# Cross attention with an adapter on one core: the wait of the turns of Wq, halves of columns in the last text unit, and a new order of all operations

## The chip, the cores and the metric

The kernel runs on one core of a Trainium2 chip. A core has five engines with instruction streams of their own: TensorE (PE in the profile, its weight loads are PEld), VectorE (DVE), ScalarE (ACT), GpSimd (POOL) and SyncE (SP), which here only issues DMAs. ACT and POOL issue DMAs too. Each engine works through its stream in order; semaphores hold it until what it needs is done. The metric is the device time of one execution in microseconds, the median of several. Lower is better.

## The reference

All is fp32. x is (2, 2048, 640), the context is (2, 128, 384): 124 text tokens and 4 adapter tokens `ca` for each batch. There are 8 heads of 80.

```python
enc, ca = context[:, :124], context[:, 124:]
query = x @ Wq                                    # (2, 2048, 640)
hs = mha(query, enc @ Wk, enc @ Wv)               # text: 2048 queries, 124 keys
ca_q1 = einsum('btc,th->bch', ca, Wq_ca)[:, indices]   # 384 rows spread over 2048
ca_hs1 = mha(ca_q1, x, x)                         # adapter: attention over all rows of x
ca_q2 = ca_hs1 @ Wq
ca_hs2 = mha(ca_q2, ca @ Wk_ca, ca @ Wv_ca)       # 4 keys
out = (hs + ca_hs2) @ Wout + b_out + x
```

`mha` is softmax(q k^T / sqrt(80)) v in each head. `indices` is `linspace(0, 383, 2048)` cut to integers, so that only 384 different rows of the adapter's query exist.

## The kernel before, in words

**Operations and their order.** The kernel is written as some 80 generators. Each yields operations `Do(engine, fn, after, needs, frees, marks)`: a function that emits the instructions, the events that it waits for (`after`), the buffers that it takes and gives back, and the events that it sets. A generator may start another one with `Fork`. The class `Desk` emits the operations, all pinned in program order on their engine. In which order is written in a table, `TURNS` (L85): for each generator, by its path in the tree of forks, the turn numbers of its operations. The smaller turn goes first, and the turn modulo 6 names the engine: 0 PE, 1 ACT, 2 DVE, 3 POOL, 4 SP, 5 none (bookkeeping). The numbers of the table were found by a search outside of the kernel; the costs that `Desk` adds up (`spent`, `COLD`, `ENTER`, `EXIT`) have no part in the order at run time, only in which of several free buffers is taken.

**Helpers.** `matmul` (L396) issues one product. `by_columns` (L405) issues one product as four strips of 32 columns of its weights, tiles of 128x32, which run side by side on the array. `transpose` (L410) turns a 128x128 block on PE. Nearly all operations of DVE, ACT and POOL are issued by one helper at L427, all DMAs of SP and ACT by `dma` (L447); so the profile's lines are told apart by the names of the tiles.

**The start.** Path `.2`, `idle_work`, is 15 dummy operations of PE (`unread<-zeros`) that keep it busy until data is there. Path `.4`, `first_loads`: SP loads the four first rows of tiles of x (`xz`, 320 KB each), then `wqca`, the context (`ctx_sb`, 384 KB) and the weights `w_kca` and `Wk`; ACT loads Wq in five chunks (`.4.1`, `of_wq`; chunks 0 and 1 are a DMA of 320 KB each, 2 and 3 are two DMAs each, the last is five small ones). Path `.6`, `x_first`, turns these first 512 rows of x on PE (`pt_x`), with copies between on DVE (`.6.1` to `.6.4`, `first_rows<-xz`, five for each tile row) and copies out of PSUM (`.6.5` to `.6.11`, `xt<-pt_x`). Path `.3` builds masks and small loads on POOL, `.5` turns the context (`pt_ctx`), and `.8`, `queries(0)`, multiplies the first 512 rows with Wq (`pq<-xt,wq_sb`), the first chunk in sets of 128 columns for the first two tile rows, everything else with 256 columns or more. Loads of further rows of x (`xi`, path `.20`, `x_load`) are SP's, from the place where `xz` was.

**The turns of Wq.** Path `.9`, `wq_turned` (L1072), needs Wq transposed, block by block. DVE first regathers the columns of the last chunk into `wq4` (`wq<-wq_sb`, two copies), which waits for all five chunks; then for each of the five row chunks i, PE turns blocks 0 to 3 from chunk i of `wq_sb` (`c0 = 0`) and block 4 from `wq4` (`c0 = 4`). All ten turns wait for `wq4`.

**The middle.** The adapter (`.55`, batch 0, and `.55.1`, batch 1) goes over its 2048 keys twice in 24 steps. In each, PE writes scores `s` into the one PSUM buffer of four banks that it has; in the first pass DVE reduces them to their maximum (`mx<-s`), in the second ACT takes the exponential (`ea<-s`), and only then can PE write the next `s`. Between the scores PE does other work: queries, and the 16 text units (`.56` to `.71`, 256 rows of x each): scores `sc`, softmax on DVE, ACT and POOL, the product with the values (`ph`), and the output product.

**The output of a text unit.** `text_out_fast` multiplies 256 rows with Wout in a scheme that saves one of eight products by sums of blocks (`hs` and `wout_sums`). It has four chains over a PSUM bank each: chain 0 of four steps, chain 1 of two, chains 2 and 3 of one step of three products, all 320 columns wide (`HALF`). After a step DVE adds the bank to a half of a tile of rows (`x_more` or `last_rows`, which hold x + b_out), two tiles of 128 rows for each unit. For all units but the last, POOL then adds the adapter's part by an indirect gather (`add_second`, L2351), and SP or ACT stores the tile, 320 KB. In the last unit (`m == UNITS - 1`, path `.71`) the gather-add comes first, and each half of a tile, 160 KB, is stored as soon as its sums are done (`stored_half`).

## Time and profile before

| | |
|---|---|
| median of 3 runs | 573.56 us (573.53 to 573.89) |
| the profiled execution | 572.92 us |
| its span, first to last instruction | 570.9 us |
| granted clock of TensorE | 1.000 |
| PE busy | 563.0 us, 8069 instructions |
| DVE, ACT, POOL busy | 394.5, 287.1, 160.1 us |
| moved by DMA | 113.21 MB, mean 198 GB/s |

The span is 2.0 us shorter than the time of its execution. The profile's page gives busy times by engine, the span in 40 slices, the chain of work that ended last, and groups of instructions. A line of the timeline reads: start, duration, engine, line of the kernel, operation, written tile <- read tiles, shape, number of instructions, and in brackets how long the engine was idle before and what released it. A line of the stages reads: the stretch, its length, then busy time and number of instructions of PE, PEld, DVE, ACT and POOL, the granted clock, the DMA share and GB/s. A line of the transfers ends with the size of one and the median us from issue to landing.

### The profile page before, as it was taken

The numbers are of one execution on the slowest core, as the hardware profiler recorded it, in microseconds if no ns is written. First come the engines' busy times: TensorE is split into PE (matmuls) and PEld (weight loads), VectorE is DVE, ScalarE is ACT, GpSimd is POOL, SyncE is SP. The second block draws the span as 40 slices with busy tenths as digits, with TensorE's granted clock in tenths as the row PEclk, the third lists the DMA queues.
The fourth block names the chain that finished last, engine by engine and source line by source line (L and its number), as shares of the span: only waits on it lengthen the run. The fifth ranks groups of instructions, "written<-read, shape, count | busy, mean of one in ns | idle before, by whom it ended". The sixth has DMA issues, their size and how long they took to land.

```text
span 570.9 us, 18875 instructions
## 1 busy us (share of the span) xinstructions
PE 563.0 (99%) x8069; PEld 309.6 (54%) x8069; DVE 394.5 (69%) x659; ACT 287.1 (50%) x806; POOL 160.1 (28%) x213
## 2 busy tenths in 40 slices
PE   8999999999999999999999999999999999999997
PEld 8885335455555455466554554555555554455553
DVE  4366999999998577458999999998332213544443
ACT  2021355645566899899885754534554664100000
POOL 9102041114440731100004350531203053045152
PEclk9999999999999999999999999999999999999999
DMA  8998476965968977446646979987476587788888
GB/s 245 219 239 141 125 160 154 175 179 133 209 214 153 221 177 214 149 123 201 228 153 201 328 187 316 224 241 228 94 248 131 167 185 243 251 217 212 255 182 209
DMA packets 145691, 113.21 MB, mean 198 GB/s; under 512 B 82548, under 2 KB 116980, under 8 KB 145608
## 3 DMA queue, kind: packets, MB, share of 16 engines
q1 hardware_dynamic: 137144, 95.43, 59.9%
q0 software_dynamic: 5632, 10.69, 11.6%
q10 hardware_dynamic: 2832, 5.90, 3.0%
q8 instruction: 63, 1.03, 0.8%
q14 instruction: 20, 0.16, 0.1%
HBM read 71.60 MB, written 40.39 MB: 196 GB/s over the span
## 4 chain that ended last, share of the span: by engine, by line
PE 93%; ACT 3%; DVE 3%; DMA 1%; issue 0%; SPq 0%; ACTq 0%
PE po L405 28%; PE pq L405 24%; PE sc L396 8%; PE acc L396 7%; PE ph L396 7%; PE s L396 7%; PE pq L396 4%; PE pyz L396 2%; ACT ea L427 2%; PE pv L396 1%; DVE mx L427 1%; PE pk L396 1%; DMA xz<-in_x_dram 1%; ACT p L427 1%; PE pt_wq L410 1%; PE pw L396 0%
## 5 line engine op out<-in xcount | busy, mean ns | idle before, releaser
L427 ACT ACTIVATE p<-sc,m 128x124 f32<-128x124 f32 x256 | 90.4, 382 | 43.0 <-DVE m L427 38.0
L427 DVE TENSOR_REDUCE mx<-s 128x4 f32<-128x2048 f32 x48 | 109.0, 2270 | 1.9 <-PE s L396 1.9
L427 ACT ACTIVATE ea<-s 128x2048 f32<-128x2048 f32 x48 | 90.5, 1886 | 30.9 <-PE s L396 30.5
L405 PE MATMUL po<-wout_sums,hs 128*32 128x320 f32 x1024 | 78.4, 434 | 0.1
L405 PE MATMUL po<-wout_sb,hs 128*32 128x320 f32 x928 | 72.3, 433 | 0.0
L427 POOL TENSOR_TENSOR p<-p,r 128x992 f32<-128x992 f32 x17 | 31.4, 1849 | 130.9 <-DVE r L427 130.9
L405 PE MATMUL pq<-xt,wq_sb 128*32 128x256 f32 (+1 forms) x928 | 66.4, 418 | 0.0
L427 DVE TENSOR_TENSOR last_rows<-last_rows,po 128x320 f32<-128x320 f32 x60 | 28.0, 480 | 44.0 <-PE po L405 43.8
L427 ACT ACTIVATION_READ_ACCUMULATOR p<-sc,m 128x1 f32 x256 | 57.2, 223 | 0.0
L427 DVE TENSOR_TENSOR x_more<-x_more,po 128x320 f32<-128x320 f32 x68 | 32.3, 480 | 34.2 <-PE po L405 33.7
L405 PEld LDWEIGHTS po<-wout_sums,hs 128*32 128x32 f32 x1024 | 33.4, 110 | 32.7 <-issue 2.7
L427 DVE TENSOR_REDUCE m<-sc 128x4 f32<-128x496 f32 x64 | 40.7, 661 | 14.1 <-PE sc L396 14.0
L396 PE MATMUL acc<-ea,y_sb 128*32 128x384 f32 (+2 forms) x768 | 50.2, 382 | 0.2 <-ACT ea L427 0.2
L396 PE MATMUL ph<-pT,vpad 128*32 128x256 f32 x768 | 47.7, 381 | 0.0
L405 PEld LDWEIGHTS po<-wout_sb,hs 128*32 128x32 f32 x928 | 30.1, 110 | 28.3 <-issue 1.6
L2351 POOL DMA_INDIRECT x_more<-o,query x17 | 26.6, 1564 | 65.2 <-DVE x_more L427 31.1
L405 PEld LDWEIGHTS pq<-xt,wq_sb 128*32 128x32 f32 x928 | 27.7, 110 | 28.0 <-issue 13.5
L427 ACT COPY hs<-ph 128x512 f32<-128x512 f32 (+1 forms) x25 | 13.4, 552 | 57.7 <-PE ph L396 57.7
L427 DVE STREAM_TRANSPOSE eb<-p 128x1024 f32<-128x1024 f32 x32 | 39.4, 1232 | 1.2 <-POOL p L427 1.1
L396 PEld LDWEIGHTS sc<-kmain,q 64*128 64x128 f32 x512 | 31.8, 187 | 12.6 <-issue 5.8
L427 POOL TENSOR_TENSOR hs<-hs 128x256 f32<-128x256 f32 x31 | 28.9, 1020 | 33.7 <-ACT hs L427 25.4
L396 PE MATMUL sc<-kmain,q 64*128 64x124 f32 x512 | 38.0, 285 | 0.0
(219 smaller groups left out, 834.4 us busy)
## 6 DMA issues: line engine op xcount, KB each, us to landing
kept<-eb SPq DMA_DIRECT2D x32, 512.0 KB, 3.5
pT<-kept SPq DMA_DIRECT2D x16, 1024.0 KB, 8.0
landing<-away SPq DMA_DIRECT2D x15, 512.0 KB, 4.8
xi<-in_x_dram SPq DMA_DIRECT2D x56, 128.0 KB, 4.2
x_more<-in_x_dram SPq DMA_DIRECT2D x17, 320.0 KB, 5.0
last_rows<-in_x_dram SPq DMA_DIRECT2D x15, 320.0 KB, 4.8
y<-yt SPq DMA_DIRECT2D x16, 256.0 KB, 3.9
y_sb<-y SPq DMA_DIRECT2D x32, 128.0 KB, 4.0
```

Of the source, the lines that this page charges most:

```text
L396: self.pin(self.nc.tensor.matmul(out, lhsT, rhs, **kw))
L405: self.pin(self.nc.tensor.matmul(out[j : j + 32], lhsT[:, j : j + 32], rhs, **kw))
L410: self.pin(self.nc.tensor.transpose(out, in_, ident))
L427: self.pin(getattr(engine, what)(*args, **kw))
L2351: desk.pin(nc.gpsimd.indirect_dma_start(out=t, out_offset=None, in_=o2_of[b], in_offset=bass.IndirectOffsetOnAxis(ap=query[:, st : st + 1] ...
```

## The change

It has three parts. First, `wq_turned` forks the regathering into a path of its own (`.9.1`, the copies out of PSUM become `.9.2` to `.9.11`), and a turn of blocks 0 to 3 of chunk i waits for chunk i alone; turns of block 4 still wait for `wq4`. Second, in the last text unit the chains of one step (2 and 3) are split into two parts of 160 columns with a bank, an add and events of their own; of the first tile (i = 0) the stores are in quarters of 160 columns (80 KB), of the second tile in halves as before. With it the paths under `.71.3` are: `.9` to `.12` quarter stores of tile 0, `.13` and `.14` half stores of tile 1, `.15` chain 0, `.16` chain 1, `.17` and `.18` the parts of chain 2, `.19` and `.20` those of chain 3. Third, all numbers of `TURNS` are new. The number of dummies is 15 in both tables. Of the table the diff below keeps the start (`.1` to `.9`), the adapter of batch 1 where turns 8448 to 9984 lie, units 8 (`.64`) and 15 (`.71`); of the rest, the two operations that stand between scores 8460 and 8532 are 8478 (a pair of output products of `.56`) and 8496 (scores of `.69.2`), and between 9900 and 9960 stand 9918 (scores of `.71.2`) and 9936 (a pair of output products of `.61`).

```diff
     TURNS = {
-        ".1": [1025], ".2": [44, 59, 60, 84, 96, 108, 114, 120, 126, 132, 150, 174, 198, 210, 234, 1002], ".3":
-        [638], ".4": [5, 52, 76, 82, 94, 106, 352, 400, 424], ".4.1": [37, 67, 169, 241, 265], ".5": [492, 523, 552,
-        565, 588, 614, 620], ".6": [11, 17, 144, 162, 204, 222, 258, 294, 300, 329], ".6.1": [140], ".6.2": [188],
-        ".6.3": [218], ".6.4": [284], ".6.5": [157], ".6.6": [194], ".6.7": [229], ".6.8": [253], ".6.9": [278],
-        ".6.10": [314], ".6.11": [319], ".7": [290, 528, 548, 1052], ".8": [23, 29, 35, 180, 246, 270, 306, 360,
-        390, 408, 438, 450, 480, 510, 558, 606, 666, 732, 792, 803], ".8.1": [416], ".8.2": [434], ".8.3": [536],
...
-        6518, 6524, 6596, 6640], ".64.2.2": [6542, 6572, 6577, 6613, 6667, 6685, 6704, 6788, 6818, 6856], ".64.3":
-        [6959, 12845, 12874, 13134, 13146, 13212, 13223], ".64.3.1": [13154], ".64.3.2": [13171], ".64.3.3":
-        [13249], ".64.3.4": [13226], ".64.3.5": [13310], ".64.3.6": [13328], ".64.3.7": [13359], ".64.3.8": [13511],
-        ".64.3.9": [13523, 13527, 13684], ".64.3.10": [13493, 13497, 13588], ".64.3.11": [13284, 13304, 13344,
-        13382, 13392, 13448, 13464, 13484], ".64.3.12": [13296, 13334, 13404, 13460], ".64.3.13": [13368, 13424],
-        ".64.3.14": [13476, 13514], ".65.1": [11836, 12010], ".65.2": [6708, 7266], ".65.2.1": [6758, 6770, 6781,
...
-        10003, 10009, 10039, 10706, 10718, 10742, 10780], ".71.3": [10853, 10883, 10894, 11052, 11142, 11262,
-        11273], ".71.3.1": [11089], ".71.3.2": [11192], ".71.3.3": [11336], ".71.3.4": [12062], ".71.3.5": [11745],
-        ".71.3.6": [11762], ".71.3.7": [12579], ".71.3.8": [13661], ".71.3.9": [13547, 13549], ".71.3.10": [13625,
-        13630], ".71.3.11": [13649, 13651], ".71.3.12": [13673, 13678], ".71.3.13": [13452, 13472, 13530, 13568,
-        13590, 13610, 13632, 13664], ".71.3.14": [13578, 13598, 13602, 13640], ".71.3.15": [13500, 13538],
-        ".71.3.16": [13554, 13616], ".72": [1517, 1772, 1802, 1832, 1904, 1976, 2030, 2177, 2522, 2630], ".73":
+        ".1": [851], ".2": [44, 59, 60, 78, 90, 102, 108, 114, 120, 138, 156, 252, 264, 348, 492, 810], ".3": [620],
+        ".4": [5, 52, 70, 76, 88, 100, 346, 358, 382], ".4.1": [37, 163, 175, 211, 235], ".5": [486, 523, 558, 572,
+        594, 614, 626], ".6": [11, 17, 126, 168, 180, 216, 246, 258, 270, 311], ".6.1": [134], ".6.2": [152],
+        ".6.3": [194], ".6.4": [242], ".6.5": [145], ".6.6": [206], ".6.7": [199], ".6.8": [230], ".6.9": [295],
+        ".6.10": [289], ".6.11": [284], ".7": [428, 528, 554, 920], ".8": [23, 29, 35, 186, 222, 276, 300, 360, 390,
+        408, 438, 450, 462, 510, 564, 600, 660, 780, 828, 839], ".8.1": [422], ".8.2": [415], ".8.3": [541], ".8.4":
+        [692], ".8.5": [989, 991, 1100, 1195, 1244], ".8.5.1": [1168], ".8.5.2": [1282], ".8.5.3": [1325], ".8.5.4":
...
+        7207], ".55.1": [5973, 6469, 7004, 7266, 7322, 7422, 7478, 7524, 7598, 7656, 7694, 7806, 7838, 7878, 7910,
+        8010, 8042, 8160, 8210, 8268, 8366, 8460, 8492, 8532, 8684, 8796, 8840, 8922, 8966, 9024, 9098, 9138, 9164,
+        9228, 9260, 9354, 9398, 9438, 9470, 9534, 9584, 9630, 9692, 9744, 9830, 9900, 9926, 9960, 10046, 10116,
+        10142, 10181, 10191, 10238, 10248, 10280, 10302, 10322, 10333, 10358, 10373, 10374, 10405, 10422, 10477,
+        10512, 10549, 10614, 10639, 10674, 10699, 10770, 10789, 10812, 10837, 10860, 10891, 10968, 10987, 11058,
...
+        11400, 11612], ".63.3.12": [11334, 11354, 11460, 11480], ".63.3.13": [11556, 11588], ".63.3.14": [11652,
+        11696], ".64.1": [13102, 13120], ".64.2": [6378, 6492], ".64.2.1": [6404, 6422, 6433, 6445, 6487, 6499,
+        6554, 6560, 6608, 6646], ".64.2.2": [6530, 6536, 6571, 6601, 6613, 6655, 6746, 6770, 6800, 6832], ".64.3":
+        [6929, 12761, 12772, 13176, 13194, 13236, 13247], ".64.3.1": [13202], ".64.3.2": [13220], ".64.3.3":
+        [13274], ".64.3.4": [13286], ".64.3.5": [13256], ".64.3.6": [13280], ".64.3.7": [13292], ".64.3.8": [13517],
+        ".64.3.9": [13469, 13473, 13654], ".64.3.10": [13529, 13533, 13729], ".64.3.11": [13296, 13340, 13374,
+        13418, 13440, 13454, 13482, 13520], ".64.3.12": [13308, 13328, 13446, 13502], ".64.3.13": [13410, 13460],
+        ".64.3.14": [13350, 13370], ".65.1": [11674, 11926], ".65.2": [6684, 7230], ".65.2.1": [6728, 6758, 6763,
+        6781, 6787, 6811, 6824, 6944, 6980, 7012], ".65.2.2": [7286, 7310, 7315, 7351, 7411, 7465, 7550, 7575, 7640,
...
+        ".71.2.1": [9650, 9674, 9679, 9697, 9709, 9727, 9884, 9897, 9992, 10024], ".71.2.2": [9956, 9968, 9973,
+        9997, 10003, 10033, 10352, 10501, 10628, 10726], ".71.3": [10805, 10913, 10924, 11154, 11160, 11274, 11285],
+        ".71.3.1": [11174], ".71.3.2": [11258], ".71.3.3": [11318], ".71.3.4": [12554], ".71.3.5": [11289],
+        ".71.3.6": [12249], ".71.3.7": [12578], ".71.3.8": [13709], ".71.3.9": [13571, 13576], ".71.3.10": [13685,
+        13690], ".71.3.11": [13643, 13648], ".71.3.12": [13613, 13666], ".71.3.13": [13721, 13723], ".71.3.14":
+        [13697, 13702], ".71.3.15": [13476, 13490, 13536, 13550, 13578, 13604, 13614, 13676], ".71.3.16": [13494,
+        13628, 13656, 13712], ".71.3.17": [13542, 13562], ".71.3.18": [13632, 13670], ".71.3.19": [13596, 13622],
+        ".71.3.20": [13554, 13586], ".72": [1553, 1772, 1802, 1880, 1904, 2066, 2102, 2111, 2468, 2552], ".73":
+        [6233, 8417], ".74": [7043, 8513], ".75": [8087, 8099, 8315, 9953], ".76": [8081, 8303], ".76.1": [8150],
...
@@ -1072,7 +1073,7 @@
 
     def wq_turned():
 
-        yield Do("DVE", lambda: columns(wq_sb, wq4), [("wq", c) for c in range(5)], marks=["wq4"])
+        yield Fork(one(Do("DVE", lambda: columns(wq_sb, wq4), [("wq", c) for c in range(5)], marks=["wq4"])), 2)
         for i in range(NCH):
             if i < 4:
                 op = yield Do("NONE", lambda at: wide_rows[at[0]], [], needs=[(first_rows, 1)])
@@ -1089,7 +1090,7 @@
                         transpose(pt[:, (c - c0) * P : (c - c0 + 1) * P], wq_of(i, c), ident)
                     return pt
 
-                op = yield Do("PE", turn, ["wq4"], needs=[(banks, 1)])
+                op = yield Do("PE", turn, ["wq4" if c0 else ("wq", i)], needs=[(banks, 1)])
                 yield Fork(one(evacuate(
                     wqT[i][:, c0:c1],
                     op.value[:, : (c1 - c0) * P].rearrange("p (c s) -> p c s", s=P),
@@ -2443,19 +2444,20 @@
             (((s4, w[1][1], (0, 1)), [("hs", m, "s4")] + end_h, ((0, 1),)),),
         )
 
-        def chain(n, steps):
+        def chain(n, steps, part=None):
 
             po, s, at = None, None, []
+            cols = slice(0, HALF) if part is None else slice(part * HALF // 2, (part + 1) * HALF // 2)
             for k, ((x, y, plus), after, ((i, u),)) in enumerate(steps):
 
                 def product(s=None, k=k, x=x, y=y, plus=plus):
-                    to = bank(s[0], f"po_{m}_{n}") if s else po
+                    to = bank(s[0], f"po_{m}_{n}_{part}") if s else po
                     pairs = [(x[:, c], y[:, c]) for c in range(2)] if x is not None else []
                     if plus:
                         pairs.append((last[plus[0]], five[plus[1]]))
                     for c, (l, r) in enumerate(pairs):
                         by_columns(
-                            to[:, :HALF], l, r, start=(k == 0 and c == 0), stop=(c == len(pairs) - 1),
+                            to[:, cols], l, r[:, cols], start=(k == 0 and c == 0), stop=(c == len(pairs) - 1),
                             skip_group_check=True,
                         )
                     return to
@@ -2467,43 +2469,52 @@
                     po, s = op.value, op.slots[0][0]
                 end = k == len(steps) - 1
                 if end:
-                    desk.event(("chain", m, n)).t = op.at.t
+                    desk.event(("chain", m, n, part or 0)).t = op.at.t
 
                 def add(i=i, u=u, po=po):
-                    t = xr_of[m][i][0][:, u * HALF : (u + 1) * HALF]
-                    desk.b_tensor_tensor(t, t, po[:, :HALF], ALU.add)
+                    t = xr_of[m][i][0][:, u * HALF : (u + 1) * HALF][:, cols]
+                    desk.b_tensor_tensor(t, t, po[:, cols], ALU.add)
 
                 op = yield Do(
-                    "DVE", add, [op.at], frees=[(banks, s)] if end else [], marks=[("sum", m, i, u, n)], rank=1
+                    "DVE", add, [op.at], frees=[(banks, s)] if end else [], marks=[("sum", m, i, u, n, part or 0)],
+                    rank=1,
                 )
                 at = [op.at]
 
-        reads = {(i, u): [] for i in range(2) for u in range(2)}
+        reads = {(i, u, v): [] for i in range(2) for u in range(2) for v in range(2)}
+        apart = [n for n, steps in enumerate(chains) if len(steps) == 1 and m == UNITS - 1]
         for n, steps in enumerate(chains):
             for _, _, (place,) in steps:
-                reads[place].append(("sum", m, *place, n))
+                for v in range(2):
+                    reads[(*place, v)].append(("sum", m, *place, n, v if n in apart else 0))
         yield Fork(one(Do(
-            "NONE", lambda: None, [("chain", m, n) for n in range(len(chains))], frees=[(hss, at_hs)]
+            "NONE", lambda: None,
+            [("chain", m, n, v) for n in range(len(chains)) for v in ((0, 1) if n in apart else (0,))],
+            frees=[(hss, at_hs)],
         )), 0)
         for i in range(2):
             if m < UNITS - 1:
-                yield Fork(stored(m, i, reads[i, 0] + reads[i, 1]), 1)
+                yield Fork(stored(m, i, reads[i, 0, 0] + reads[i, 1, 0]), 1)
             else:
                 for u in range(2):
-                    yield Fork(stored_half(m, i, u, reads[i, u]), 1)
+                    for v in range(2) if i == 0 else (None,):
+                        yield Fork(stored_half(m, i, u, v, reads[i, u, 0] + reads[i, u, 1] if v is None else reads[i, u, v]), 1)
         for n, steps in enumerate(chains):
-            yield Fork(chain(n, steps), 30 + m)
+            for part in (0, 1) if n in apart else (None,):
+                yield Fork(chain(n, steps, part), 30 + m)
 
     fast_of = {}
 
-    def stored_half(m, i, u, ends):
+    def stored_half(m, i, u, v, ends):
 
         b, st = tiles(m)[i]
         cols = slice(u * HALF, (u + 1) * HALF)
+        if v is not None:
+            cols = slice((2 * u + v) * HALF // 2, (2 * u + v + 1) * HALF // 2)
         yield Do("NONE", lambda: None, ends)
         t = xr_of[m][i][0]
         to = out[b, st * P : (st + 1) * P, cols]
-        yield Do(("SP", "ACT"), lambda: dma(to, t[:, cols], 0.43, 0.45, 2.2))
+        yield Do(("SP", "ACT"), lambda: dma(to, t[:, cols], 0.43 if v is None else 0.25, 0.45, 2.2))
 
     def stored(m, k, both):
 
```

## The prediction

> **What bounds the kernel now.** I read the page first, then the stages, the waits of PE, and the timeline of the two ends, because a change of order can only win where PE is not already working.

> ```profile
> span 570.9 us, 18875 instructions
> PE 563.0 (99%) x8069; PEld 309.6 (54%) x8069; DVE 394.5 (69%) x659; ACT 287.1 (50%) x806; POOL 160.1 (28%) x213
> ```

> PE is busy for 563.0 of the span's 570.9 us. Most of the 7.9 us left lie at one end or the other:

> ```profile
> 0.00:5.00 5.00, 3.65 (x18) 3.49 (x19) 0.44 (x3) 1.28 (x1) 4.36 (x35) 1.00 0.60 204
> 565.00:571.00 6.00, 1.71 (x28) 0.67 (x19) 1.56 (x4) 0.00 (x0) 0.00 (x0) 0.98 0.62 240
> PE s L396 <- DVE mx L427: 1.1, 2, 0.7
> PE s L396 <- ACT ea L427: 0.6, 3, 0.2
> ```

> The first two lines are stages (length, then busy time of PE, PEld, DVE, ACT, POOL): 1.35 us of PE are free in the first 5 us, 4.29 us after 565. The last two are what PE waited for in between: the adapter's scores s wait for their one PSUM buffer, 1.1 us behind the reduction mx on DVE and 0.6 us behind the exponential ea on ACT. So the kernel is its PE instructions, a start of some 10 us, a tail of 4.3 us and under 2 us of stalls. The diff takes no product away.

> **The wait on Wq.** The timeline of the start:

> ```profile
> 0.81 0.90 ACTq L447 DMA_DIRECT2D wq_sb<-in_L_xattn_Wq_dram  x2
> 1.13 3.48 PE L396 MATMUL unread<-zeros 128*128 128x128 f32 x16 [1.13 <-DVE zeros L427]
> 4.73 0.64 DVE L427 COPY first_rows<-xz 128x64 f32<-128x64 f32 x5 [3.65 <-DMA xz<-in_x_dram]
> 5.29 1.17 ACTq L447 DMA_DIRECT2D wq_sb<-in_L_xattn_Wq_dram  x2
> 5.86 1.41 POOL L427 MEMSET vpad<- 128x768 f32 x2
> 6.19 1.86 DVE L427 COPY first_rows<-xz 128x64 f32<-128x64 f32 x5 [0.82 <-DMA xz<-in_x_dram]
> 6.75 0.39 PE L396 MATMUL unread<-zeros 128*128 128x128 f32 x2
> 6.97 0.38 PE L410 MATMUL pt_x<-ident,xz 128*128 128x128 f32 x2
> 7.39 0.37 ACT L427 COPY xt<-pt_x 128x256 f32<-128x256 f32 x1 [1.74 <-PE pt_x L410]
> 8.54 1.06 PE L396 MATMUL pq<-xt,wq_sb 128*128 128x128 f32 x8
> 9.43 0.38 PE L410 MATMUL pt_x<-ident,xz 128*128 128x128 f32 x2
> 9.87 1.89 PE L396 MATMUL pq<-xt,wq_sb 128*128 128x256 f32 x8
> 12.25 5.34 PE L396 MATMUL pq<-xt,wq_sb 128*128 128x256 f32 x24
> 14.34 1.31 DVE L427 COPY wq<-wq_sb 128x320 f32<-128x320 f32 x2 [1.41 <-DMA wq_sb<-in_L_xattn_Wq_dram]
> 17.43 2.32 PE L396 MATMUL pq<-xt,wq 128*128 128x256 f32 x10
> 21.32 0.60 PE L410 MATMUL pt_wq<-ident,wq_sb 128*128 128x128 f32 x4
> 23.49 0.38 PE L410 MATMUL pt_ctx<-ident,ctx_sb 128*128 128x128 f32 x2
> ```

> The relaxed wait is worth nothing by itself. wq4, which the turns waited for, was ready at 14.34+1.31 = 15.65, and the first turn ran at 21.32 because PE had products in front of it until then. In the new table the first turn is still the 29th PE operation (it was the 30th): one set of four products earlier.

> **The start in its new order.** Three things differ. ACT now issues chunk 1 of Wq after its first copy of xt, at about 5.29 and not right behind chunk 0 at 0.81, so 320 KB stand no longer ahead of x rows 1 to 3. POOL clears vpad after its 16 small loads instead of at 5.86: the five DVE copies of row 1 took 1.86 us under those memsets, where row 0's took 0.64. And PE puts all turns of x before the 256-column products, with seven dummies ahead of the first turn where there were eight, two between the last turns, and two (turns 348 and 492) later.

> Step by step: ACT's second copy of xt now stands behind three issues, 5.29 + 0.45 + 1.17 = 6.91 (0.45: half of the 0.90 that the two issues at 0.81 took), and ends at 7.28. The second set of 128-column products may start then; the set takes 9.43-8.54 = 0.89: 8.17. Ten turns at 0.11 (four of them from 9.43 to 9.87, the first two shown) and two dummies at 0.22 (6.75 to 6.97) make 1.54: 9.71. Four sets of 256 columns at (17.43-12.25)/3 = 1.73 and the dummy of turn 348: 16.85 against 17.43, 0.58 us won. The dummy of turn 492 gives 0.22 back: **0.36 us won** before the context turns. What this hangs on is when chunk 1 lands:

> ```profile
> xz<-in_x_dram SPq DMA_DIRECT2D x4, 320.0 KB, 5.4
> wq_sb<-in_L_xattn_Wq_dram ACTq DMA_DIRECT2D x4, 160.0 KB, 4.3
> ctx_sb<-in_ctx_dram SPq DMA_DIRECT2D x1, 384.0 KB, 6.1
> ```

> Issued at 5.29, with 4.3 us it lands at 9.6, just in time; with the 5.4 us of the x rows at 10.7, and the start loses 0.6 us instead. The other end, with no queue ahead of ACT's copy, is some 1.1 us won. I take 0.4 won, nearest to the 4.3 us row because ctx is no longer in the queue: SP has it behind the first loads of xi now, into buffers that come free with row 3's turns, at 9.7 by the sum above. With 6.1 us to land, ctx may be issued as late as 17.4 for its reader at 23.49: that is its cover.

> **The tiles of PE.** Counted along PE's order in the two tables, the array changes its tiling 259 times before and 262 times after. What one costs:

> ```profile
> 342.72 0.72 PE L405 MATMUL po<-wout_sb,wout_sums 128*32 128x320 f32 x8
> 343.26 1.26 PE L405 MATMUL po<-wout_sb,hs 128*32 128x320 f32 x16
> 344.45 0.51 PE L396 MATMUL s<-zop,cop 32*128 32x512 f32 x4
> ```

> Eight instructions take 0.54 us up to the next of their own form (342.72 to 343.26), so sixteen take 1.08; up to another form they take 1.19 (343.26 to 344.45): 0.11 each, so **+0.33 us** (ends 0 and 0.5). [...]

> **The halves.**

> ```profile
> 31.63 1.02 PE L396 MATMUL p_kca<-w_kca,cadT 128*32 128x160 f32 x24
> L396 PE MATMUL p_kca<-w_kca,cadT x24: 299/299/323, 31.6 to 32.4; 128*32 128x160 f32 x24
> ```

> Of 160 columns, 24 instructions are six passes of four strips: (1.02-0.30)/5 = 0.144 us a pass at most, against 0.27 for 320 (0.54 above is two passes). Two chains of six passes become 24 half passes: 24 x 0.144 - 12 x 0.27 = +0.2 at most, 0 at least; I take **+0.1**. Two more DVE adds lie beside PE.

> **The tail.**

> ```profile
> last_rows<-o,query POOLq DMA_INDIRECT x3, 6.1
> 565.42 1.29 PE L405 MATMUL po<-wout_sb,hs 128*32 128x320 f32 x16
> 566.23 1.03 DVE L427 TENSOR_TENSOR x_more<-x_more,po 128x320 f32<-128x320 f32 x2 [0.61 <-PE po L405]
> 566.74 0.34 ACTq L447 DMA_DIRECT2D out_dram<-x_more  x1
> 567.28 0.33 SPq L447 DMA_DIRECT2D out_dram<-x_more  x1
> 567.71 0.41 SPq L447 DMA_DIRECT2D out_dram<-last_rows  x1
> ```

> PE ends at 566.71, the last add at 567.26 (two in 1.03 us), the last half store is issued at 567.28, and behind it on SP stands the 320 KB store of unit 8's first tile, at 567.71. That one ends the span. After the change the last PE operation is an uncut one, the three products of chain 1 (turn 13656), its add is 320 columns wide, its store is uncut on ACT (13723), and behind it on ACT stands the store of unit 8's other tile (13729). The same links, 0.52 + 0.34 + 0.41 and a landing: the quarters leave earlier, but nothing that ends last is cut. The gather-add of that tile follows turn 13482, after which 16 products at 0.54 are left, 8.6 us. The gather-adds of the last 16 us took 6.1 us from issue to landing (the row of the transfers above): in time by 2.5 us, unless two queue up. **0**, ends -0.4 (the store no longer behind the half) and +0.5.

> **The middle.** In the stretch of the adapter PE's order is nearly the old one, and what stands between one scores operation and the next is the same at the two worst places:

> ```profile
> 309.61 0.51 PE L396 MATMUL s<-zop,cop 32*128 32x512 f32 x4 [0.45 <-DVE mx L427]
> 310.98 2.23 DVE L427 TENSOR_REDUCE mx<-s 128x4 f32<-128x2048 f32 x1
> 313.26 0.50 PE L396 MATMUL s<-zop,cop 32*128 32x512 f32 x4 [0.66 <-DVE mx L427]
> ```

> The cycle is the scores, 2.23 us of mx and whatever DVE does before mx (0.86 here, 310.98 less 310.12). Those stalls I take as they are. But at two other places the work between gets shorter. Between turns 8460 and 8532 stand now one pair of output products and one text score: 1.08 + 0.92 (the 16 instructions from 311.04 to 311.96) + three changes of tiling = 2.3, where 8 stood before; between 9900 and 9960 the same 2.3, where 2.9 stood. mx with its two hand-overs of 0.05 takes 2.33 (313.26 is 0.05 behind its end), so PE waits there for as long as DVE is late: 0 at least, 0.86 each at most. DVE has two adds ahead of mx at either place, most of which can run under the work before: 0.15 each, nearer to the low end because both mx stand right behind them, **+0.3** (ends of the middle: -1.7, all that mx and ea cost, and +1.7).

> **Sum.** -0.4 + 0.33 + 0.1 + 0 + 0.3 = +0.3 us on the profiled execution of 572.92 (span 570.9 and 2.0 around it): 573.2. The median of the runs is 0.6 above that execution, so I forecast **573.9**, no change that can be told.

> **The rivals.** *Faster: the stalls go.* DVE's order is rearranged around mx too. If the waits of s fall, the 1.7 us and the 0.3 that I add, the time is 571.9. For it: these are the only stalls that the trace names in the middle. Against: PE's work between the worst scores is the same, 2.6 us (310.04 to 312.60), under the cycle.

> *Slower: the adapter's buffer, at the two new places.* At 0.86 us each, 1.7 us and not 0.3, the time is 575.3. It decides from 0.55 us each on. For it: 0.86 is what the trace shows nearby. Against: those adds wait for products that are done before the scores.

> [...]

> *Not what it says:* the relaxed wait moves nothing, 573.9 still; that is part of my forecast.

> **How the numbers follow.** Within 0.2% (1.15 us, about what a measurement of this kernel tells from no change; 572.4 to 574.7): 0.52, the forecast. The faster rival 0.18, with the early end of the start and of the tail 0.04 more: 0.22. The adapter's buffer 0.15, a cold start 0.03, chunk 1 late together with some stall 0.08: 0.26. The range takes in both ends of the middle and 0.3 us of the start and the tiling each way: 571.9 - 0.3 = 571.6 and 575.3 + 0.3 = 575.6. The forecast's own is 572.8 to 574.7.

> **What would show it.** The first 256-column products near 9.7, wq<-wq_sb near 14, pt_wq still beyond 20; five copies of row 1 within 1 us; PE's last product 3.6 to 4.4 us before the span's end, and an out_dram<-last_rows on ACT as the last issue; the waits of s still 1 to 2 us. The forecast is wrong if PE waits for wq_sb near 10 us, if a new name heads PE's waits, or if the tail is under 3.6 us.

## The result and the profile after

The changed kernel takes 576.48 us (median of five, 575.73 to 577.56), beside 573.56 us for the kernel before in the same batch: a ratio of 1.0052, with a 95% interval of 1.0037 to 1.0066. It is slower by 2.9 us; the forecast was no change at 573.9, and its range ended at 575.6. The profiled execution of the changed kernel took 577.56 us (span 575.8), 4.64 us more than the one of before (572.92, span 570.9). Two slow executions, one of 937.99 us in `e4_code_only` and one of 590.78 in `e8_start_after`, are in the medians below but not in the ratios; without them the medians are 573.88 and 575.09.

Helpers and lines of the changed kernel stand one line further down (L397 for L396, and so on). From the page of the changed kernel, and then its table of what PE waited for (us in total, number of times, longest):

```profile
span 575.8 us, 18968 instructions
PE 564.0 (98%) x8117; PEld 307.8 (53%) x8117; DVE 390.3 (68%) x659; ACT 283.5 (49%) x796; POOL 163.4 (28%) x218
```

```profile
PE po L397 <- DVE mx L428: 1.2, 1, 1.2
PE unread L397 <- DVE zeros L428: 1.1, 1, 1.1
PE s L397 <- DVE mx L428: 1.0, 2, 0.8
PE pv L397 <- DVE first_rests L428: 0.9, 1, 0.9
PE s L397 <- ACT ea L428: 0.6, 3, 0.2
PE po L397 <- DVE o L428: 0.5, 1, 0.5
PE pyz L397 <- DVE wq_sums L428: 0.5, 1, 0.5
PE pt_x L411 <- DMA xz<-in_x_dram: 0.3, 1, 0.3
PE acc L397 <- ACT ea L428: 0.2, 1, 0.2
```

The 1.1 us of `unread` stand at the very start of both kernels. Without them the waits of this table sum to 5.2 us; the table of before has 2.5 (the 1.1 and 0.6 shown with the prediction, and 0.4, 0.2 and 0.2 in three other rows). A new name heads the list, `po <- mx`; a new name there was one of the prediction's signs that it is wrong. The 4.64 us divide into 2.7 of waits, 1.0 of PE's own time (564.0 against 563.0), 0.76 behind PE's last product (570.59 to 577.56 is 6.97, before 566.71 to 572.92 was 6.21) and 0.2 in gaps that no row names.

The larger waits in the timeline of PE all stand at places where the prediction had none (of the smaller ones, the 0.45 for `wq_sums` is at 198 us and a 0.20 of `s` at 150):

```profile
58.99 1.88 PE L397 MATMUL pv<-w_v,ctxT 128*128 128x320 f32 x6 [0.88 <-DVE first_rests L428]
68.12 0.50 PE L397 MATMUL s<-zop,cop 32*128 32x512 f32 x4 [0.80 <-DVE mx L428]
298.03 0.82 PE L397 MATMUL po<-w_sb,p2T 32*128 32x320 f32 x8 [1.22 <-DVE mx L428]
496.19 0.81 PE L397 MATMUL po<-w_sb,p2T 32*128 32x320 f32 x4 [0.51 <-DVE o L428]
```

DVE's timeline gives the reason of the first two (the upper rows) and of the third (the lower rows):

```profile
57.92 0.71 DVE L428 STREAM_TRANSPOSE xt<-xi 128x512 f32<-128x512 f32 x1 [4.54 <-DMA xi<-in_x_dram]
58.55 0.39 DVE L428 TENSOR_TENSOR first_rests<-pq,first_rests 128x256 fp32r<-128x256 f32 x1
...
60.10 2.28 DVE L428 TENSOR_REDUCE mx<-s 128x4 f32<-128x2048 f32 x1
...
293.88 1.23 DVE L428 STREAM_TRANSPOSE eb<-p 128x1024 f32<-128x1024 f32 x1
295.04 0.64 DVE L428 TENSOR_TENSOR q<-q,pq 128x512 f32<-128x512 f32 x1
295.61 2.27 DVE L428 TENSOR_REDUCE mx<-s 128x4 f32<-128x2048 f32 x1
```

In the new order the transpose of a load, `xt<-xi`, stands on DVE ahead of the add of `first_rests` and of the first `mx`. It waited 4.54 us for its load, and everything behind it waited too: `mx` ran at 60.10. In the kernel before, `mx` stood ahead of the transpose (58.30) and ran at 56.09:

```profile
56.09 2.29 DVE L427 TENSOR_REDUCE mx<-s 128x4 f32<-128x2048 f32 x1 [0.94 <-PE s L396]
```

At 298 it is the adapter's one PSUM buffer again, but the operation that waits is not a score: `po<-w_sb,p2T`, the second product of the adapter, takes the same four banks. In the new order `eb<-p` and an add stand ahead of `mx` on DVE, so `mx` ends at 297.88 where PE wanted the buffer at 296.81. In the kernel before, `mx` had ended at 293.43 and the same product did not wait:

```profile
293.58 0.82 PE L396 MATMUL po<-w_sb,p2T 32*128 32x320 f32 x8
```

At 496 only 16 products (1.08 us) stand between two such `po`, where 32 stood.

Two waits of before are gone, as the rows of the same two scores show, which have no bracket now (they were 0.45 and 0.66 us):

```profile
310.36 0.51 PE L397 MATMUL s<-zop,cop 32*128 32x512 f32 x4
313.52 0.50 PE L397 MATMUL s<-zop,cop 32*128 32x512 f32 x4
```

So the middle won 1.1 us at 310 and lost 1.2 at 298.

### The profile page after: what moved, and what is told of

Its sections match the earlier page's. It is cut to its first block, busy times and chain, and to the rows that moved or that the text cites. A ratio compares the mean times of both kernels' runs of the same rounds, so it can differ in the third digit from the quotient of the medians.

```text
span 575.8 us, 18968 instructions
## 1 busy us (share of the span) xinstructions
PE 564.0 (98%) x8117; PEld 307.8 (53%) x8117; DVE 390.3 (68%) x659; ACT 283.5 (49%) x796; POOL 163.4 (28%) x218
## 4 chain that ended last, share of the span: by engine, by line
PE 78%; DVE 12%; DMA 3%; ACT 3%; issue 1%; SPq 1%; DVEq 0%; ACTq 0%
PE po_None L406 27%; PE pq L406 14%; PE ph L397 7%; PE acc L397 7%; PE s L397 6%; PE sc L397 5%; DVE mx L428 5%; PE pq L397 4%; PE pyz L397 2%; ACT ea L428 2%; DMA xi<-in_x_dram 2%; DVE xt L428 1%; DVE m L428 1%; PE pk L397 1%; SPq L448 1%
## 5 line engine op out<-in xcount | busy, mean ns | idle before, releaser
L406 PE MATMUL po_None<-wout_sums,hs 128*32 128x320 f32 x1024 | 78.8, 434 | 0.0
L428 POOL TENSOR_TENSOR p<-p,r 128x992 f32<-128x992 f32 x17 | 32.4, 1907 | 157.3 <-DVE r L428 157.3
L406 PE MATMUL po_None<-wout_sb,hs 128*32 128x320 f32 x880 | 68.6, 434 | 0.0
L428 DVE TENSOR_TENSOR x_more<-x_more,po_None 128x320 f32<-128x320 f32 x68 | 31.9, 480 | 49.6 <-PE po_None L406 46.5
L428 ACT ACTIVATION_READ_ACCUMULATOR p<-sc,m 128x1 f32 x256 | 59.1, 232 | 0.0
L428 DVE TENSOR_TENSOR last_rows<-last_rows,po_None 128x320 f32<-128x320 f32 x58 | 27.3, 483 | 41.2 <-PE po_None L406 41.2
L397 PE MATMUL acc<-ea,y_sb 128*32 128x384 f32 (+2 forms) x768 | 50.8, 383 | 0.2 <-ACT ea L428 0.2
L406 PEld LDWEIGHTS po_None<-wout_sums,hs 128*32 128x32 f32 x1024 | 31.8, 110 | 33.0 <-issue 3.5
L397 PE MATMUL ph<-pT,vpad 128*32 128x256 f32 x768 | 47.4, 380 | 0.0
L428 POOL TENSOR_TENSOR hs<-hs 128x256 f32<-128x256 f32 x37 | 30.9, 923 | 55.6 <-ACT hs L428 41.8
L406 PEld LDWEIGHTS po_None<-wout_sb,hs 128*32 128x32 f32 x880 | 27.0, 110 | 28.0 <-issue 1.9
L2352 POOL DMA_INDIRECT last_rows<-o,query x15 | 23.5, 1567 | 53.0 <-DVE last_rows L428 42.4
L397 PEld LDWEIGHTS sc<-kmain,q 64*128 64x128 f32 x512 | 31.6, 187 | 12.9 <-issue 6.4
L397 PE MATMUL sc<-kmain,q 64*128 64x124 f32 x512 | 37.7, 284 | 0.0
```

Of the source, the lines that this page charges most:

```text
L397: self.pin(self.nc.tensor.matmul(out, lhsT, rhs, **kw))
L406: self.pin(self.nc.tensor.matmul(out[j : j + 32], lhsT[:, j : j + 32], rhs, **kw))
L428: self.pin(getattr(engine, what)(*args, **kw))
L2352: desk.pin(nc.gpsimd.indirect_dma_start(out=t, out_offset=None, in_=o2_of[b], in_offset=bass.IndirectOffsetOnAxis(ap=query[:, st : st + 1] ...
```

## The experiments

There are two theories. **The order**: the loss comes from the new order, as waits of PE at the places above, each caused by what DVE has in front. **The code**: the halves and quarter stores cost it. The first leaves a question: are the waits single places that can be mended, or does a mended wait move on to the next link?

**The changed kernel once more** (`e1_again`), no edit:

> The changed kernel once more, for a second trace. Theory (the order of DVE and PE at four places sets the loss): the same waits at the same places, pv near 59 us 0.9, s near 68 us 0.8, po<-w_sb,p2T near 298 us 1.2 and near 496 us 0.5, each within 0.3 us; time 575.7 to 577.2. Rival (the loss is made by transfers that land at other times in each execution): these four waits differ from the first trace by more than 0.5 us in sum, and the spread of the times comes from them. What lies behind PE's last product, 5.2 us in the first trace, may differ under both.

576.02 us, ratio 1.0055 (1.0035 to 1.0074). Its profiled execution took 575.19. The waits of PE, and DVE at the load:

```profile
PE po L397 <- DVE mx L428: 1.2, 1, 1.2
...
PE ph L397 <- DMA pT<-kept: 0.6, 1, 0.6
```

```profile
54.62 0.71 DVE L428 STREAM_TRANSPOSE xt<-xi 128x512 f32<-128x512 f32 x1 [1.10 <-DMA xi<-in_x_dram]
...
56.81 2.27 DVE L428 TENSOR_REDUCE mx<-s 128x4 f32<-128x2048 f32 x1
```

The same program, and here the load came 3.3 us earlier: no wait at 59 and none at 68. The waits of 1.22 (here at 296) and 0.51 (at 495) are the same to the hundredth; the 0.6 for `pT` is a transfer that was late in this execution and not in that of 577.56. So two of the four waits stand in both executions and belong to the order, and two depend on when a load lands. Of the small ones the 0.20 of `s` is here too (at 149), the 0.45 of `pyz` is not. Theory and rival each have a part: the four waits sum to 3.41 and 1.73 us, which differs by more than the rival's 0.5, and still the medians are 576.48 and 576.02. How long SP stands at three loads of `xi` near 41 us differs as well:

```profile
41.52 5.98 SPq L448 DMA_DIRECT2D xi<-in_x_dram  x3
```

That is the execution of 577.56; here the same three took 3.67 us. Among the runs below that have this start, `e8_start_after`, with the load early (54.70), has 3.36 us, and `e2_mx_first`, `e5_two_places` and `e6_order_only`, with the load late (57.66 to 59.12), have 6.88, 5.08 and 6.56. In the kernel before, where DVE's `mx` does not stand behind the load, it is 4.69. The stand alone does not decide: in `e10_wout_later` it is 2.01 and the load is used at 56.05.

**`mx` ahead of the load** (`e2_mx_first`). On DVE:

```diff
+1286 mx<-s, 1244 first_rests<-pq,first_rests
 1238 xt<-xi
-1244 first_rests<-pq,first_rests, 1286 mx<-s
```

> The changed kernel with two operations of DVE moved: the first mx of the adapter and one addition of first_rests go ahead of the first transpose xt<-xi of rows 1024 to 1535, as the mx stood before the change. Theory (DVE waits 4.5 us for that load with mx and the addition behind it): the waits of pv near 59 us and of s near 68 us go, 1.7 us in all, time 574.4 to 575.1 where the changed kernel has 576.5. Rival (the load itself comes too late, whatever stands in front of it): the wait moves to the next reader of xt, time within 0.4 us of the changed kernel's.

576.06 us, 1.0037 (1.0025 to 1.0049). The load was late again (the transposes at 59.12), `mx` ran at 55.48, and the waits at 59 and 68 were gone. In their place:

```profile
62.25 1.92 PE L406 MATMUL pq<-xt,wq_sb 128*32 128x512 f32 x16 [0.61 <-ACT vpad L428]
```

With another 0.26 us at 73.41, for `q` on ACT, half of the 1.68 moved on. The median is that of `e1_again`; the ratio is lower than its 1.0055, but the intervals overlap, so that a gain is not shown.

**All three places** (`e3_three_places`): `e2_mx_first`, and

```diff
 7656 s
+7694 mx<-s, 7640 eb<-p
 7664 q<-q,pq
-(7640 eb<-p ahead of 7664, 7694 mx<-s behind it)
+12306 pair of output products
 12300 po<-w_sb,p2T
-12306 pair of output products
```

> As the kernel before this one, and two places more: near 298 us the mx of DVE directly behind its scores (a transpose and an addition go behind it), and near 496 us one pair of output products of PE ahead of the second po<-w_sb,p2T. Theory (po of the adapter's second product uses the same PSUM buffer as the scores): 1.2 and 0.5 us less than with the first place alone, time 572.8 to 573.6. Rival (the wait moves to the scores behind po, since DVE's work is the same): no more than 0.5 us less, 574.2 or more.

578.12 us, 1.0083 (1.0064 to 1.0102): worse, where 572.8 to 573.6 was expected. The wait at 496 went. At 298 my edit had put the add of `q` behind `mx`, and PE's next product waits for this add, which reads `pq` out of PSUM and gives the bank back:

```profile
296.03 1.94 PE L406 MATMUL pq<-xt,wq_sb 128*32 128x256 f32 x16 [2.64 <-DVE q L428]
297.90 1.45 PE L397 MATMUL po<-w_sb,p2T 32*128 32x320 f32 x8
299.28 3.13 PE L406 MATMUL pq<-x_sums,wq_sb 128*32 128x256 f32 x32
```

The stall is 2.64 us. The scores ahead of it (291.40) stand 1.23 us behind those of the kernel before (290.17), the scores behind it (302.34) 6.15 behind (296.19): against the kernel before, the stretch lost 4.9 us. The products themselves are slow: 3.13 us for 32 that take 1.93 elsewhere. The stages in steps of 1 us show why, by the granted clock (the third number from the end):

```profile
294.00:295.00 1.00, 0.00 (x0) 0.00 (x0) 1.00 (x2) 0.00 (x0) 0.00 (x0) 0.97 0.00 0
295.00:296.00 1.00, 0.00 (x0) 0.00 (x0) 1.00 (x3) 0.00 (x0) 0.00 (x0) 0.50 0.00 0
...
301.00:302.00 1.00, 1.00 (x16) 0.50 (x12) 1.00 (x1) 1.00 (x7) 0.00 (x0) 0.62 0.15 56
```

The clock fell to half in the stall and stayed there for 5.7 us of work behind it.

**The code parts alone, old order** (`e4_code_only`): the changed code, with the table of before; where one operation became two, both stand at its place.

```diff
 (code of the changed kernel)
-TURNS of the change
+TURNS of the kernel before
```

> The code of the change (the relaxed wait of the turns, the halves of columns, the quarter stores) in the old order of all operations, each half directly behind the other. Theory (all of the loss is the order's): 573.4 to 574.0, as before the change. Rival (the halves and the quarter stores cost at the end): 574.2 or more, with more than 4.6 us behind PE's last product.

574.05 us, 1.0011 (1.0001 to 1.0021). Waits as before: 1.1, 0.6 and 0.2. By the ratio the code costs some 0.6 us of the 2.9 (0.0011 x 573; by the interval, 0.1 to 1.2).

**The last two places, mended otherwise** (`e5_two_places`): the changed kernel with the edit at 496 of `e3_three_places`, and at 298

```diff
 7656 s
+7664 q<-q,pq, 7694 mx<-s, 7640 eb<-p
-(7640 eb<-p, 7664 q<-q,pq, 7694 mx<-s)
```

> The changed kernel with two places mended, the start left as it is: near 298 us the mx of DVE right behind the two additions q<-q,pq, with the transpose eb<-p behind it; near 496 us one pair of output products of PE ahead of the second po<-w_sb,p2T. Theory (po shares the PSUM buffer of the scores, so it waits for DVE): the waits of 1.2 and 0.5 us go, PE's last product 1.5 to 1.8 us earlier than in the changed kernel with the same start, time 574.2 to 574.8. Rival (DVE is full there, the wait only moves on to the scores behind po): 575.4 or more.

576.66 us, 1.0051 (1.0027 to 1.0075). The wait of `po` fell from 1.22 to 0.18, the one at 496 went, and the next score waits:

```profile
296.76 0.82 PE L397 MATMUL po<-w_sb,p2T 32*128 32x320 f32 x8 [0.18 <-DVE mx L428]
300.41 0.50 PE L397 MATMUL s<-zop,cop 32*128 32x512 f32 x4 [0.97 <-ACT o L428]
```

0.18 + 0.97 is 1.15 of the 1.22, and a further product waits 0.20 behind it: the buffer is passed from `mx` to `po`, from `po` to the copy `o` and on to the next score, and only the place of the wait changed. The 0.51 at 496 went without a new wait behind it, here and in `e3_three_places`; in the times it does not show.

**The order alone, old code** (`e6_order_only`): the kernel before with the table of the change; where two operations are one, it stands at the later place.

```diff
 (code of the kernel before)
-TURNS of the kernel before
+TURNS of the change
```

> The code of before (old wait of the turns, no halves, half stores) in the new order of all operations. Theory (the quarter stores and halves cost what the code alone cost in the old order, 0.4 to 0.7 us; the rest is the order's): 575.3 to 575.8 and 4.0 to 4.5 us behind PE's last product. Rival (the last stores on ACT cost it, which are the order's): as the changed kernel, 576.0 or more, with 4.6 us or more behind PE's last product.

577.05 us, 1.0064 (1.0044 to 1.0084). Its waits of PE:

```profile
PE po L396 <- DVE mx L427: 1.2, 1, 1.2
...
PE po L405 <- DVE x_more L427: 1.0, 1, 1.0
PE pv L396 <- DVE first_rests L427: 0.7, 1, 0.7
```

By the ratio the new order costs 3.7 us (0.0064 x 574) without a line of the new code. The 1.0 us of `po <- x_more` is this experiment's own, likely since one chain stands uncut at a place made for two halves. The 2.7 left are most of the 2.9.

**The old order with the new one from 290 to 315** (`e7_hybrid`): old code and old order up to the first score of batch 1 (`.55.1`, 3), then the new order with both edits of `e5_two_places` to the output stage (`.55.1`, 61), then the old one. It asks whether the 1.1 us that went at 310 can be had alone.

```diff
 (code of the kernel before)
 TURNS of the kernel before, up to .55.1, 3
-TURNS of the kernel before, .55.1, 3 to .55.1, 61
+TURNS of the change, .55.1, 3 to .55.1, 61, with both edits
 TURNS of the kernel before
```

> The code of before; its own order up to the first scores of batch 1 (277 us), from there the new order with the place near 298 us mended, up to the second pass of batch 1 (396 us), and the old order behind that. Theory (in the new order the two waits of s at 309 and 313 us, 1.1 us in all, are gone, and nothing else in this stretch costs once po waits no longer): 572.3 to 572.9, under before. Rival (what the new order wins at 309 us it gives back by later waits in the same stretch): 573.3 or more.

574.61 us, 1.0012 (1.0004 to 1.0021). The two waits at 310 are gone, and in their place a score waits 0.97 us at 297.30 for `o` on ACT, and two products 0.19 and 0.18. Nothing was won; by the ratio 0.7 us were lost.

**The new start alone** (`e8_start_after`): new code, new order up to `.55`, 23, an operation of the adapter's first steps, old order behind it.

```diff
 (code of the changed kernel)
 TURNS of the change, up to .55, 23
-TURNS of the change
+TURNS of the kernel before
```

> The code of the change; the new order up to the eleventh scores (104 us), the old order from there. Theory (at the start DVE stands in front of a load of x that lands at other times in each execution, so that the loss there is 0.3 us at least and up to 2.1): against the code alone in the old order 0.3 to 1.5 us more in the median and a wider spread, 574.3 to 575.6. Rival (the first trace was an accident, the start costs nothing): within 0.3 us of the code alone, 573.8 to 574.3.

575.18 us, 1.0039 (1.0019 to 1.0059). Its profiled execution, 575.27, had the load early and no wait of PE between 5 and 100 us; other executions reach 577 to 581, where those of `e4_code_only` end at 575.3. So the new start has a spread that the old one lacks, also with nothing new behind it. This execution shows one more thing that moves the start:

```profile
5.12 1.06 PE L397 MATMUL unread<-zeros 128*128 128x128 f32 x4
```

Four products take 0.86 us here, up to the next at 5.98. That is the slow pace of the first dummies, 0.21 each; in the profiled execution of the changed kernel the same four, at 5.20, take 0.50 up to 5.70, and at the full pace it is 0.11 each. The first clock record of a trace, of 1.00, begins at 4.17 us in the kernel before, where the dummies go over from 0.21 to 0.11 each, at 5.31 in the changed kernel and at 7.17 here; I read it as the rise of the clock. Over all fourteen profiled executions it lies between 4.17 and 7.17, in either order. In the three of the new start that rise near 7 us (`e5_two_places`, here and `e10_wout_later`) the context turns come at 23.87 to 23.94, where the changed kernel has 23.41 and `e1_again`, with 6.28, has 23.56. In the old order it is 24.01 with a rise at 7.06 (`e11_mx_sooner`), and 23.43 to 23.51 in five executions with a rise up to 6.16. So a late rise costs either start about 0.5 us.

**The old start, then the new order** (`e9_old_start`): new code, old order up to `.55`, 9, new order behind it.

```diff
 (code of the changed kernel)
-TURNS of the change, up to .55, 9
+TURNS of the kernel before, up to .55, 9
 TURNS of the change
```

> The code of the change; the old order up to the fourth scores (70 us), the new order from there: the counterpart of the kernel with the new start alone. Theory (the start costs 0.3 to 2.1 us, the rest of the new order 1.2 to 1.9): no wait of pv at 59 us or of s at 68 us, 574.8 to 575.6 with a narrow spread. Rival (all of the loss comes from the start): 574.3 or less, as the code alone in the old order.

576.81 us, 1.005 (1.0037 to 1.0063). No wait at 59 or 68, but where the orders meet:

```profile
82.69 1.52 PE L397 MATMUL sc<-kmain,q 64*128 64x124 f32 x14 [1.00 <-ACT q L428]
```

and 1.22 at 297 and 0.51 at 495 as in the changed kernel. It does not price the start alone, since the joint has a wait of its own.

**The loads of Wout later** (`e10_wout_later`): in the changed kernel SP issues the two large loads of Wout (turns 682 and 700) behind the load of `xi` of turn 1144, to clear the queue ahead of `xi`.

```diff
-682 wout_sb<-Wout, 700 wout_sb<-Wout
 1144 xi<-in_x
+682 wout_sb<-Wout, 700 wout_sb<-Wout
```

> The changed kernel with the two large loads of Wout moved on SP's queue from in front of the loads of x rows 1024 to 1535 to behind them. Theory (SP stands for 2.2 to 5.7 us at the third of those loads, behind what was issued before): the last of them is issued before 52 us and DVE's first xt<-xi of these rows starts before 55 us, the waits near 59 and 68 us go in this execution too; 575.0 to 575.6 in the median, and the highest time under 576.5. Rival (the loads are held up by what was issued before Wout): xt<-xi starts at 57 us or later in some executions, times as the changed kernel's.

577.04 us, 1.0067 (1.004 to 1.0094). DVE took up the late `xi` at 56.05, between the 54.62 and the 57.92 of the two executions of the changed kernel; the waits at 59 and 68 were gone, and a wait for `q` stands at 75:

```profile
75.27 1.64 PE L397 MATMUL sc<-kmain,q 64*128 64x124 f32 x12 [2.52 <-ACT q L428]
```

On ACT the cast of `krest` had waited 4.07 us for its load `k_parts`, and the copy of `q` stood behind it: the same pattern as on DVE, with another load. That is an execution of 582.41 us; a second took 583.04, the other six 576.2 to 577.4. A later Wout does not mend the start, and since `xi` lands early or late by itself, one profile does not say whether this edit moved it.

**Two DVE operations sooner in the kernel before** (`e11_mx_sooner`), to take away the two waits at 309 and 313 us that the prediction shows:

```diff
+8222 mx<-s
 8192 (.54.8, 5)
-8222 mx<-s
+8048 mx<-s
 7982 eb<-p
-8048 mx<-s
```

> The kernel before with two operations of DVE moved: the transpose eb<-p behind the mx of the scores at 306 us, and the mx of the scores at 309.6 us ahead of one addition of wq_sums. Theory (s at 309.6 and 313.3 us waits because of what DVE does in front of mx): the two waits fall from 1.1 us to 0.2, time 0.6 to 0.9 us under before, 572.6 to 573.2. Rival (what is put behind mx is late for its own readers): a new wait of pT or of a bank, 573.5 or more.

578.81 us, 1.0087 (1.0074 to 1.01). The two waits of the scores went, and the text scores wait instead:

```profile
311.66 0.48 PE L396 MATMUL sc<-kmain,q 64*128 64x124 f32 x2 [0.59 <-ACT hs L427]
314.03 1.25 PE L396 MATMUL sc<-kmain,q 64*128 64x124 f32 x10 [1.89 <-DVE wq_sums L427]
```

The stretch lost 5.5 us where the two waits together are 2.5: the clock again, below. This edit does not take out the 1.1 us of before.

**The halves without the quarter stores** (`e12_halves_only`), old order:

```diff
-                    for v in range(2) if i == 0 else (None,):
+                    for v in (None,):
```

> The code of the change in the old order as before, but the last unit's first tile is stored in two halves and not in four quarters; the products of chains 2 and 3 stay in halves of columns. Theory (the 0.6 us of the code alone are the quarter stores'): 573.4 to 573.8. Rival (they are the halved products', by PE or by DVE's additions): 573.9 to 574.3.

573.79 us, 1.0004 (0.9995 to 1.0013). The halves cost nothing that can be told. `e4_code_only`, which has the quarter stores too, stands 0.07% above, 0.4 us, with intervals that overlap.

## Why the prediction was wrong

**The step that failed** is the middle and the start as I costed them: "In the stretch of the adapter PE's order is nearly the old one, and what stands between one scores operation and the next is the same at the two worst places". I compared the order of PE, and from one score to the next. Three things were not in that comparison.

- The order of DVE in front of a load. I followed the start up to the turns of the context at 23 us and priced nothing between there and the adapter's first scores. There `xt<-xi` had been moved ahead of `first_rests` and `mx`: 0.88 + 0.80 us in the profiled execution, nothing in the one of `e1_again`. The change adds no wait there, it moves two operations behind one that waits.
- A third user of the adapter's PSUM buffer. I counted `s`, read by `mx` and `ea`; the second product `po<-w_sb,p2T` takes the same banks. 1.22 us at 298 and 0.51 at 496, in the changed kernel, `e1_again`, `e6_order_only` and `e9_old_start` alike.
- Small ones of the same kind: a score at 150, 0.20 in every run with the new order there, and `pyz` for `wq_sums`, 0.45 in the changed kernel and 0.48 in `e2_mx_first`, but not in `e1_again`, `e5_two_places` or `e6_order_only`.

With these terms, 0.3 for the middle would have been 1.22 + 0.51 + 0.45 + 0.20 - 1.11 = +1.3 by rows of the result (0.8 without the 0.45), and the start +1.7 or 0 by the load. With the 0.4 of the tail below, that is 1.2 to 3.4 us, around the 2.9 of the medians.

**Part by part.** *The wait on Wq:* worth nothing by itself: `e12_halves_only` contains it, with the old order, and stands 0.1 us from before (573.79 against 573.68); it contains the halves too. *The start:* the first 256-column products came at 10.00 where 9.7 was forecast, and the context turns at 23.41 where they were at 23.49:

```profile
10.00 3.62 PE L397 MATMUL pq<-xt,wq_sb 128*128 128x256 f32 x16
13.46 0.39 PE L397 MATMUL unread<-zeros 128*128 128x128 f32 x2
13.68 3.85 PE L397 MATMUL pq<-xt,wq_sb 128*128 128x256 f32 x16
17.36 2.32 PE L397 MATMUL pq<-xt,wq 128*128 128x256 f32 x10
...
23.41 0.38 PE L411 MATMUL pt_ctx<-ident,ctx_sb 128*128 128x128 f32 x2
```

0.08 us were won. I had also misread one place: the dummy of turn 492, for which I took 0.22 off, stands behind the first context turns (turn 486), so that my sum for this point was 0.58 and not 0.36. Of it, 0.3 went because the first set came late, and 0.22 because the sixteen instructions from 13.68 took 3.68 us up to 17.36 where those from 10.00 took 3.46. In `e2_mx_first` PE waits 0.40 us there for `wq_sb`, so a chunk of Wq can arrive at the last moment, as I feared for chunk 1; `wq<-wq_sb` ran at 15.56 where I had 14. Part of the lateness is likely the clock of this one execution, which rose 1.1 us later than in the kernel before (4.17 and 5.31): with rises at 6.25 (`e2_mx_first`) and 7.17 (`e8_start_after`) the first set comes at 10.31 and 10.76. *The tilings:* three more, as counted; 0.33 us is too little to be seen. PE's busy time is 563.9 with the new order (`e1_again`, `e6_order_only`) and 563.9 with the old one (`e12_halves_only`), where the profile of before had 563.0: one execution resolves no better than 1 us here, and the 1.0 of "PE's own time" above need not be the order's. *The halves:* +0.1 forecast, none measured. Twenty-four instructions of 160 columns take 0.82 us (566.62 to 567.44), so four such sets 3.28, against 12 x 0.27 = 3.24. *The tail:* 0 was forecast, its ends -0.4 and +0.5, and PE's last product 3.6 to 4.4 us before the end of the span; it was 5.2.

```profile
566.62 1.00 PE L406 MATMUL po<-wout_sb,hs 128*32 128x160 f32 x24
...
567.44 0.72 PE L406 MATMUL po_None<-wout_sb,hs 128*32 128x320 f32 x8
...
569.87 0.72 PE L406 MATMUL po_None<-wout_sb,hs 128*32 128x320 f32 x8
...
570.66 0.49 DVE L428 TENSOR_TENSOR x_more<-x_more,po_None 128x320 f32<-128x320 f32 x1 [0.90 <-PE po_None L406]
571.18 0.84 ACTq L448 DMA_DIRECT2D out_dram<-x_more  x2
```

The links are those of the forecast: an uncut product, an add, two stores on ACT. From PE's last product to the end of the execution it is 6.97 us here. Over nine profiled executions with quarter stores the mean is 6.59 (6.26 to 7.02), over five with half stores 6.22 (5.90 to 6.35): +0.4, inside the ends, but at the upper one. The two groups overlap, and what in the quarter stores would cost it is not shown.

**The rivals.** *The adapter's buffer* had the right resource, the right engine in front, and nearly the time (575.3), but the wrong places: the scores at turns 8532 and 9960, which I had priced at 0.15 each, do not wait for `mx` at all: the two waits of that row are those at 68 and 150 us. So its time came near the measured one by luck. *The stalls go* came true by 1.1 us, but 1.2 us had been paid 12 us earlier, at 298; `e7_hybrid` and `e11_mx_sooner` speak against an accident of the table, since in both a wait turned up next door. *Cold start*, 0.03 in the sum of the chances: no trace shows it. The clock rises in all fourteen profiled executions, up to 3 us later than in the kernel before (4.17), at 5.31 in the changed kernel and up to 7.17 elsewhere, in the old order as well, and a late rise costs some 0.5 us; it does not make the 2.9. *Not what it says* is right for the wait on Wq. The chance of slower, 0.26, was too low and its reasons too narrow: a new order of some 2,300 operations has many places like 298, and I had judged it by the two that were already bad.

**What stays open.** Why the loads of `xi` land between 54.6 and 57.9 us in executions of one order. SP's stand at the loads near 41 us varies with it in six of the seven profiled executions of this start that show when the load was there, so a backlog of transfers is likely, but which transfer makes it was not shown, and `e10_wout_later`, the seventh, speaks for more than one cause. The landing time is likely also what spreads the changed kernel's times over 575.2 to 579.2, where the kernel before, in the same batch, lies between 572.9 and 575.1.

## What to carry to other kernels

When an order is changed, list for each engine, not for the bound one alone, what now stands in front of the operations that the bound engine waits for, and above all whether any of it waits for a transfer: in an in-order engine such an operation hands its lateness to all behind it (DVE's 4.54 us for `xi` became 0.88 and 0.80 us of PE). List all users of a buffer with one slot by its allocation, not by the name of its best-known reader. And where PE is busy for 98% of the span, as here, expect a mended wait to turn up at the next link: of six such edits (`e2`, `e3`, `e5`, `e7`, `e10`, `e11`) none made its kernel faster by more than the intervals tell, and none came under the kernel before.

## What the runs showed of the hardware

```profile
75.00:76.00 1.00, 0.73 (x6) 0.74 (x8) 1.00 (x3) 1.00 (x3) 0.04 (x1) 0.62 0.60 171
...
81.00:82.00 1.00, 1.00 (x8) 0.29 (x4) 0.00 (x0) 1.00 (x6) 0.00 (x0) 0.50 1.02 130
82.00:83.00 1.00, 1.00 (x12) 0.29 (x12) 0.65 (x1) 0.23 (x1) 0.00 (x0) 0.97 0.48 64
```

The clock records of the traces hold only 0.5 and 1, so a mean of 0.62 is a fall at 75.24 and 0.97 a rise at 82.06: 6.8 us. The same reading gives 294.94 to 301.76 in `e3_three_places`, 6.8 us as well. What of it is work takes up to twice as long (the eight `po` at 297.90 in `e3_three_places` take 1.38 us up to the next instruction, 0.75 at 293.58 in the kernel before), so by this estimate up to 3.4 us are lost beside the stall. Measured against the kernel before, the stretch lost 4.9 us for the stall of 2.64, and 5.5 for those of 0.59 and 1.89. The stall of 1.22 us at 298 in the changed kernel did not lower the clock (1.00 in each stage from 296 to 301), nor did those of 0.8 to 1.0 elsewhere (1.00 from 58 to 61 and from 68 to 70 in the changed kernel, and from 80 to 90 in `e9_old_start`). In `e3_three_places` the stall began at 293.39 (296.03 less 2.64), so the clock had fallen after 1.55 us of it. In the other two some 2.5 us of idle lay ahead of the fall. What sets its moment, and the 6.8 us, no run shows.

**One program starts in more than one way.** The loads near 41 us hold SP for 3.67 or 5.98 us in two executions of the changed kernel, and PE waits for none or for 1.7 us behind them. The clock rises 3.0 to 6.0 us after the first dummy (1.13 us), over fourteen profiled executions, and the context turns come up to 0.5 us later behind a late rise. A single profile of this kernel shows one such start.
